# An R-GCN kernel on one core: sums for groups of 512 nodes held in PSUM, and row copies issued by SyncE alone

## The chip, the core and the metric

The kernel runs on one NeuronCore of one Trainium2 chip. The metric is the time of one execution in microseconds (us), taken on the device; ten runs are shown as a median with their lowest and highest. A profile is one further execution with every instruction recorded. Engines are named PE (TensorE, the matrix engine), DVE (VectorE), ACT (ScalarE), POOL (GpSimd) and SP (SyncE, which computes nothing and issues DMAs). L12 is line 12 of the kernel before, unless the text says "of the changed kernel".

## What is computed

Two layers of a relational graph convolution over 50,000 nodes with 128 features, then a residual and a layer norm. The 850,000 edges come sorted by destination; 50,000 of them are loops (one for each node, source equal to destination), so 800,000 join two nodes. Each edge has one of 16 relations, and a relation's 128x128 matrix is a mix of 8 bases.

```python
def _rgcn_layer(h, src, dst, rel, basis, w_comp, loop_w, bias):
    W = jnp.einsum('rb,bio->rio', w_comp, basis)
    seg = dst.astype(jnp.int32) * N_REL + rel.astype(jnp.int32)
    agg = jax.ops.segment_sum(h[src], seg, num_segments=N_ENT * N_REL)
    agg = agg.reshape(N_ENT, N_REL, -1)
    msg = jnp.einsum('nri,rio->no', agg, W)
    return jax.nn.relu(msg + h @ loop_w + bias)
h = _rgcn_layer(x, ...);  h = _rgcn_layer(h, ...)
x = _layernorm(x + h)
```

## The kernel before, in words

**Tiles and chunks.** The 800,000 edges are 6,250 tiles of 128 edges, and ten tiles (K = 10) make a chunk, so a layer has C = 625 chunks. The main loop (L925) goes over the chunks, once for each of the two layers (L854); the first layer reads `x`, the second reads `H1`, the first one's result in device memory.

**Source rows.** For each tile the 128 rows `h[src]` are brought into one of five chunk buffers `g` (GATHERS = 5) by an indirect DMA that POOL issues (`gather`, L202). In chunk c the gathers of chunk c + 2 are issued (L932 to L942). The first gather into a buffer waits until PE has read all of the chunk that was in it, five chunks earlier (`read_by`, L987).

**Tiles copied row by row.** The last tile of some chunks has no gather. Its 128 rows are copied by 128 single-row DMAs of 512 bytes (`row_by_row`, L789) into a buffer `by_hand`; the row addresses are loaded from a small table into an engine's registers, 16 at a time (L798). Two engines do this, each for every eighth chunk: SP for c % 8 = 7 and ACT for c % 8 = 3 (`HANDS`, L783; `by_hand`, L785). A copy is begun nine chunks before its chunk (L943 to L946) and issued in small portions behind the matmuls (L984 to L986).

**Sums by slot.** For each tile, DVE builds `hot` (L871): for each edge, its 8 basis weights at the place of its destination among 12 consecutive nodes ("slots"). PE multiplies the gathered rows by it (L971, `pa`), so a tile leaves 8 sums of 128 features for each of its 12 slots; ACT copies five tiles at a time from PSUM to `aT` (L979). Then PE multiplies by the eight bases and adds up in PSUM (`slots`, L734: eight matmuls of 120x128 a chunk), and ACT copies the result to SBUF (L739).

**From slots to nodes.** A window of 128 nodes, which begins at the chunk's first node, is taken for each chunk. PE adds the chunk's own slots and those of the chunk before by two 0/1 matrices (`masks_of`, L753; `nodes_of`, L761), DVE adds the nodes' own part `ls` (L764), which was stored to device memory earlier (L727) and is loaded again for the window (L883), and the window is finished and stored: relu on ACT (L768) in the first layer; in the second relu and residual in one DVE instruction with both tensors in SBUF (L771), then the norm (`normed_steps`, L601 to L614) and the store. A window's start is read from a register of SP (`at`, L627, with a load of 8 registers at L630).

**The own part.** `from_itself` (L692) does it for 128 nodes at a time: transpose (L209), two matmuls of 128x512 by the eight bases (L710), weights of the loops by DVE (L713), a matmul by the loop matrix (L722), the sum over nine terms on DVE (L726) and a store (L727).

**Preparing the edge lists.** During the first layer, DVE works through ten blocks of the edge list (`runs`, L310; `loops_of`, L415; `rows_of`, L442), a step or so for each chunk; two scatters for each block are issued by POOL (L378, L434).

**What sets the order.** PE, POOL, DVE and ACT run in the order in which the code is written (L853, `manual_schedule`). SP's order is made by a scheduler. A DMA issued by SP or ACT takes one of eight completion lanes in turn and waits until the DMA that had that lane before it has landed.

At the end a count that the kernel keeps of its own assumptions (`count_up`, L548) decides whether a slow general version (`summed`, L1028) is run as well.

Of the kernel before, what the change touches and what calls it, by code (L numbers as in the profile page):

```python
# [39 lines left out]
F32 = mybir.dt.float32  # L40
# [22 lines left out]
AHEAD = 4  # L63
# [8 lines left out]
BASES = 8  # L72
BY_HAND = 8
# [8 lines left out]
def tile_rgcn_resnorm(  # L82
# [21 lines left out]
    NG, NT = -(-R // P), -(-N // P)  # L104
# [9 lines left out]
    assert D == P and N >= P and edges.shape[0] == 1 and AT * NR == P and PER * NB * WN <= BANK and AT * PER * NB == WEIGHTS and PER == HALF and S <= P and C >= 4 and M > 0 and RUN - LK // 2 == LIVE and 2 * C <= NG * P and N <= 1 << 16 and E % ROW == 0  # L114
# [11 lines left out]
    NL = -(-(N + LK) // P) * P  # L126
    LREL = dram.tile([2 * NL, 1], I32, name="LREL")

    L = [dram.tile([N, D], F32, name=f"L{n}") for n in range(2)]
# [67 lines left out]
    ps_o = ctx.enter_context(tc.tile_pool(name="ps_o", bufs=1, space=PSUM))  # L197
    ps_n = ctx.enter_context(tc.tile_pool(name="ps_n", bufs=1, space=PSUM))
    ps_h = ctx.enter_context(tc.tile_pool(name="ps_h", bufs=2, space=PSUM))
# [6 lines left out]
    def turned(h, m, sb):  # L206

        tp = ps_o.tile([P, D], F32, name="po")
        nc.tensor.transpose(tp[:, :m], h, ident[:m, :m])  # L209
        hT = sb.tile([P, P], F32, name="hT")  # L210
        nc.scalar.copy(hT[:, :m], tp[:, :m])  # L211
        return hT[:, :m]
# [8 lines left out]
    key = consts.tile([P, 2 * C * HALF], BF16, name="key")  # L221


    base_i = consts.tile([1, C], I32, name="base_i")
    slot = consts.tile([P, C], F32, name="slot")
    next_slot = consts.tile([P, C], F32, name="next_slot")
    last_slot = consts.tile([P, 1], F32, name="last_slot")
    first_of = consts.tile([1, C], F32, name="first_of")
    base1 = consts.tile([1, C], F32, name="base1")
    minus = consts.tile([1, S], F32, name="minus")  # L230
# [4 lines left out]
    picked = consts.tile([P, 5 * NG + len(ROWS) + 4], F32, name="picked")  # L235
    ones = consts.tile([P, max(LIVE, C)], F32, name="ones")
# [10 lines left out]
    nc.vector.memset(minus, -1.0)  # L247
# [5 lines left out]
    def set_up(pool):  # L253
# [14 lines left out]
        po = ps_o.tile([P, D], F32, name="po")  # L268
# [146 lines left out]
    def loops_of(g, pool, m, d_i, k_f, r_i, loop, loops, asked):  # L415
# [15 lines left out]

        nc.vector.tensor_scalar(picked[0:1, 5 * g + 4 : 5 * g + 5], d_i[0:1, 0:1], float(asked()), None, op0=OP.is_ge)
        yield
# [8 lines left out]
    def rows_of(j, pool):  # L442
# [3 lines left out]
        parts = pool.tile([P, 2, LIVE, 2], F32, name="parts")  # L446
        for h in range(2):
            nc.sync.dma_start(
                parts[:m, h],
                FULL[h * NP + r0 * LIVE : h * NP + (r0 + m) * LIVE].rearrange("(p e) w -> p e w", e=LIVE),  # L450
            )
        if j:
            yield
        srcf = pool.tile([P, LIVE], F32, name="srcf")
        nc.vector.tensor_tensor(srcf[:m], parts[:m, 0, :, 0], parts[:m, 1, :, 0], op=OP.add)
        node = pool.tile([P, LIVE], I32, name="node")
        nc.vector.tensor_tensor(node[:m], parts[:m, 0, :, 1], parts[:m, 1, :, 1], op=OP.add)
# [19 lines left out]
        placed = put(srcf, src)  # L477
        row_at = pool.tile([P, LIVE], F32, name="real").bitcast(I32)[:, :P]
# [6 lines left out]
        keyf = pool.tile([P, LIVE], F32, name="keyf")  # L485
# [6 lines left out]
        if (r0 + m) * LIVE > M:  # L492
# [6 lines left out]
                beyond[:m], place[:m, :LIVE], last[:m], 64.0, op0=OP.subtract, op1=OP.mult  # L499
# [8 lines left out]
        po = ps_o.tile([P, D], F32, name="po")  # L508
# [6 lines left out]
        nc.vector.tensor_scalar(base1[:, c0 : c0 + cs], half[0:1, :, 0], float(N - P), None, op0=OP.min)  # L515
        nc.vector.tensor_scalar(base_i[:, c0 : c0 + cs], base1[:, c0 : c0 + cs], float(4 * D), None, op0=OP.mult)

        a, b = max(c0 - 1, 0), c0 + cs - 1
        off = pool.tile([1, P], F32, name="off")
        nc.vector.tensor_tensor(off[:, : b - a], base1[:, a + 1 : b + 1], base1[:, a:b], op=OP.subtract)  # L520
        yield
        po = ps_o.tile([P, D], F32, name="po")
        for h in range(2):
            nc.tensor.matmul(po[:S, :cs], spread[h], half[:, :, h], start=h == 0, stop=False)
        nc.tensor.matmul(po[:S, :cs], minus, base1[:, c0 : c0 + cs], start=False, stop=True)
        nc.vector.tensor_scalar(slot[:S, c0 : c0 + cs], po[:S, :cs], within[:S], None, op0=OP.add)
        yield
        po = ps_o.tile([P, D], F32, name="po")
        nc.tensor.matmul(po[:, : b - a], ones[0:1, :P], off[:, : b - a], start=True, stop=True)
        nc.vector.tensor_tensor(next_slot[:S, a:b], slot[:S, a:b], po[:S, : b - a], op=OP.subtract)  # L530
        if b == C - 1:
            nc.vector.tensor_tensor(
                last_slot[:S], next_slot[:S, b - 2 : b - 1], po[:S, b - a - 1 : b - a], op=OP.subtract
            )
# [6 lines left out]
            ones[:m, :LIVE],  # L541
# [6 lines left out]
    def count_up(pool):  # L548
        last = 5 * NG + len(ROWS)
        off = pool.tile([1, C], F32, name="off_all")  # L550

        nc.vector.memset(off, float(N - 1))
        nc.vector.tensor_copy(off[:, : C - 1], first_of[:, 1:])
        nc.vector.tensor_tensor(off, off, base1, op=OP.subtract)
        nc.vector.scalar_tensor_tensor(
            off, off, float(P - 1), ones[0:1, :C], op0=OP.is_le, op1=OP.mult, accum_out=picked[0:1, last : last + 1]
        )

        in_time = pool.tile([1, C], F32, name="in_time")
        nc.gpsimd.iota(  # L560
            in_time,
            pattern=[[P * NT // C, C]],
            base=P * AHEAD - P,
# [3 lines left out]
        nc.vector.tensor_tensor(off, base1, in_time, op=OP.subtract)  # L567
        nc.vector.scalar_tensor_tensor(
            off, off, 0.0, ones[0:1, :C], op0=OP.is_le, op1=OP.mult, accum_out=picked[0:1, last + 1 : last + 2]
        )  # L570

        nc.vector.tensor_tensor(off[:, : C - 3], base1[:, 2 : C - 1], first_of[:, 1 : C - 2], op=OP.subtract)
        nc.vector.tensor_tensor(off[:, C - 3 : C - 2], base1[:, C - 1 :], first_of[:, C - 3 : C - 2], op=OP.subtract)
        nc.vector.scalar_tensor_tensor(
            off[:, : C - 2],
            off[:, : C - 2],
            1.0,
            ones[0:1, : C - 2],
            op0=OP.is_ge,
            op1=OP.mult,  # L580
            accum_out=picked[0:1, last + 3 : last + 4],
        )
        nc.vector.tensor_scalar(picked[0:1, last + 2 : last + 3], first_of[:, 0:1], 0.0, None, op0=OP.is_equal)
# [3 lines left out]
        total = ps_o.tile([P, D], F32, name="po")  # L587
# [4 lines left out]
            off[:, 1:2], total[:1, 1:2], float(E + 2 * NG * (P + 1) + 3 * C - 1), None, op0=OP.not_equal  # L592
# [3 lines left out]
    def normed(t, m, sb):  # L596

        *_, o = normed_steps(t, m, sb)
        return o

    def normed_steps(t, m, sb):  # L601
        st = sb.tile([P, 6], F32, name="st")
        nc.vector.bn_stats(st[:m], t)  # L603
        mv = sb.tile([P, 2], F32, name="mv")
        nc.vector.bn_aggr(mv[:m], st[:m])  # L605
        sd = sb.tile([P, 1], F32, name="sd")
        nc.scalar.activation(sd[:m], mv[:m, 1:2], AF.Sqrt, bias=eps[:m])  # L607
        yield
        rs = sb.tile([P, 1], F32, name="rs")
        nc.vector.reciprocal(rs[:m], sd[:m])  # L610
        nm = sb.tile([P, 1], F32, name="nm")
        nc.vector.scalar_tensor_tensor(nm[:m], mv[:m, 0:1], -1.0, rs[:m], op0=OP.mult, op1=OP.mult)  # L612
        o = sb.tile([P, D], F32, name="o")
        nc.scalar.activation(o[:m], t, AF.Identity, bias=nm[:m], scale=rs[:m])  # L614
        yield o

    def chunked():
        with (
# [8 lines left out]
            def at(c):  # L627

                if c % BASES == 0:
                    _, starts[:] = nc.values_load_multi_w_load_instructions(  # L630
                        base_i[0:1, c : min(C, c + BASES)],
                        engines=[mybir.EngineType.SP],
                        min_val=0,
                        max_val=(N - P) * 4 * D,
                        skip_runtime_bounds_check_because="bases are clamped to N - P, and no node is below 0",
                    )
                return starts[c % BASES]

            def nodes_at(of, start):
                return of.bitcast(U8).rearrange("n d -> (n d)")[ds(start, P * 4 * D)].rearrange("(p d) -> p d", p=P)  # L640

            def weights(c, n):
# [9 lines left out]
                is_rel = hp.tile([P, LIVE], F32, name="is_rel")  # L652
# [14 lines left out]
            def loop_weights(i, n):  # L667

                m = min(AT, NT - i) * NR
                rel = hp.tile([P, 2, P], I32, name="lrel")  # L670
                for h in range(2):
                    nc.sync.dma_start(
                        rel[:m, h, :],
# [18 lines left out]
            def from_itself(i, of, n, lws):  # L692
# [8 lines left out]
                if i % AT == 0:  # L701
                    lws[:] = [next(weigh)]
# [512 lines left out]
```

## Time and profile before

| what | value |
|---|---|
| median of 10 runs | 15414.09 us (15409.94 to 15418.7) |
| the profiled execution: its own time | 15411.18 us |
| its span (first to last instruction) | 15409.4 us |
| granted TensorE clock, mean | 0.809 |
| busy: PE, DVE, ACT, POOL | 75%, 44%, 16%, 75% |
| gathers on POOL | 6,096 in each layer |
| row copies | 19,712 on SP and 19,712 on ACT |

In the profile a row of a group gives line, engine, operation, tiles (out<-in), shape, count, then the busy time and the mean duration of one, and behind the second bar the engine's idle time just ahead of these instructions and what ended it. "Issue" means that the engine waited for nothing that the profile shows. A fp32 matmul appears as two records, so a count of matmul records is twice that of the matmuls.

### The profile page before, as it was taken

How to read it: one execution, taken by the hardware profiler on the slowest of the kernel's cores; microseconds unless marked ns; L12 is line 12 of the kernel's file. 1: busy time of each engine (PE TensorE's matmuls, PEld its weight loads, DVE VectorE, ACT ScalarE, POOL GpSimd, SP SyncE). 2: the span in 40 equal slices, each digit the busy share in tenths (PEclk: the TensorE clock that was granted, in tenths of full speed). 3: DMA queues.
4: the chain of work that ended last, by engine and by line, in shares of the span. 5: the costliest groups of instructions: out<-in, count | busy, mean ns of one | idle time of the engine just before them, and what ended most of it. 6: DMA issues, size and time to landing. Idle time of an engine off the chain costs nothing. (4 is left out here: it accounts for less than half of the span.)

```text
span 15409.4 us, 255870 instructions
## 1 busy us (share of the span) xinstructions
PE 11590.4 (75%) x59202; PEld 9165.9 (59%) x59202; DVE 6777.2 (44%) x14585; ACT 2520.9 (16%) x6567; POOL 11585.2 (75%) x12224
## 2 busy tenths in 40 slices
PE   6777777776777777777777777777777777777777
PEld 4656555655666555556555555656666565656556
DVE  6544544445333333333344444444444444444444
ACT  1111111111111111111111111111111111111111
POOL 6777777777777777777777777777777777777777
PEclk8787787777788888888878888787787888888887
DMA  3333333333322222222223333333333333333332
GB/s 95 83 86 86 83 85 86 80 84 80 81 75 75 75 75 75 75 74 75 74 77 80 80 80 80 80 81 80 80 81 80 81 81 80 81 79 81 79 80 75
DMA packets 1236470, 1232.33 MB, mean 80 GB/s; under 512 B 318004, under 2 KB 1028332, under 8 KB 1234940
## 3 DMA queue, kind: packets, MB, share of 16 engines
q0 software_dynamic: 393696, 806.61, 20.9%
q1 hardware_dynamic: 798604, 397.62, 9.0%
q10 hardware_dynamic: 42640, 11.62, 0.3%
q8 instruction: 481, 7.88, 0.2%
q14 instruction: 1049, 8.59, 0.2%
HBM read 1059.71 MB, written 154.87 MB: 79 GB/s over the span
## 5 line engine op out<-in xcount | busy, mean ns | idle before, releaser
L971 PE MATMUL pa<-hot,g 128*128 128x96 f32 x24384 | 5933.2, 336 | 3358.3 <-DMA g<-H,src 1641.8
L971 PEld LDWEIGHTS pa<-hot,g 128*128 128x128 f32 x24384 | 4582.7, 233 | 5732.4 <-DMA g<-H,src 2272.6
L202 POOL DMA_INDIRECT g<-in_x_dram,src x6096 | 5793.6, 950 | 1891.3 <-issue 1811.9
L202 POOL DMA_INDIRECT g<-H,src x6096 | 5765.4, 946 | 1875.5 <-issue 1833.9
L734 PE MATMUL ps<-basis,aT 128*120 128x128 f32 x20000 | 3948.9, 332 | 0.0
L734 PEld LDWEIGHTS ps<-basis,aT 128*120 128x120 f32 x20000 | 3345.5, 235 | 0.0
L979 ACT COPY aT<-pa 128x480 f32<-128x480 f32 x2500 | 1395.4, 558 | 8242.0 <-DMA by_hand<-in_x_dram 3058.2
L713 DVE TENSOR_TENSOR by<-hb,lw 128x512 f32<-128x512 f32 x1564 | 1077.1, 689 | 3703.9 <-PE hb L710 3701.9
L710 PE MATMUL hb<-basis,hT 128*128 128x512 f32 x3128 | 2114.1, 765 | 4.2 <-ACT hT L211 4.2
L726 DVE TENSOR_REDUCE ls<-by 128x128 f32<-128x1152 f32 (+1 forms) x782 | 1657.2, 2119 | 13.5
L871 DVE TENSOR_TENSOR hot<-fixed,own 128x960 f32<-128x960 f32 x1250 | 1446.7, 1157 | 62.5 <-DVE own L864 1.8
L723 DVE TENSOR_TENSOR by<-po,bias 128x128 f32<-128x128 f32 (+1 forms) x782 | 227.2, 291 | 2257.6 <-PE po L722 2219.4
L761 PE MATMUL pn<-slots,own 120*128 120x128 f32 x5000 | 970.5, 326 | 31.8 <-DVE a L764 27.2
L761 PEld LDWEIGHTS pn<-slots,own 120*128 120x128 f32 x5000 | 817.1, 232 | 35.3 <-DVE a L764 29.9
L864 DVE TENSOR_TENSOR own<-fixed,key 128x120 f32<-128x120 f32 x1250 | 342.9, 274 | 1122.8 <-PE fixed L658 1104.3
L710 PEld LDWEIGHTS hb<-basis,hT 128*128 128x128 f32 x3128 | 598.7, 238 | 7.9 <-ACT hT L211 7.9
L607 ACT ACTIVATE sd<-mv,eps 128x1 f32<-128x1 f32 x625 | 184.1, 295 | 2377.3 <-DMA by_hand<-H 1768.5
L658 PE MATMUL fixed<-each,is_rel 128*128 128x64 f32 x3140 | 507.8, 323 | 4.0 <-DVE is_rel L653 4.0
L658 PEld LDWEIGHTS fixed<-each,is_rel 128*128 128x128 f32 x3140 | 489.6, 240 | 4.7 <-DVE is_rel L653 4.4
L209 PE MATMUL po<-ident,h_own 128*128 128x128 f32 (+1 forms) x782 | 271.5, 347 | 284.1 <-ACT lw L689 227.0
L614 ACT ACTIVATE o<-a,nm,rs 128x128 f32<-128x128 f32 x625 | 308.2, 493 | 961.9 <-DMA by_hand<-H 512.4
L753 DVE TENSOR_SCALAR own<-col,slot 120x128 f32<-120x128 f32 x1250 | 407.2, 326 | 0.0
(152 smaller groups left out, 4274.2 us busy)
## 6 DMA issues: line engine op xcount, KB each, us to landing
by_hand<-in_x_dram ACTq DMA_DIRECT2D x9856, 0.5 KB
by_hand<-in_x_dram SPq DMA_DIRECT2D x9856, 0.5 KB
by_hand<-H ACTq DMA_DIRECT2D x9856, 0.5 KB
by_hand<-H SPq DMA_DIRECT2D x9856, 0.5 KB
g<-in_x_dram,src POOLq DMA_INDIRECT x6096
g<-H,src POOLq DMA_INDIRECT x6096
ls_of<-L SPq DMA_DIRECT2D x1250, 64.0 KB
L<-ls SPq DMA_DIRECT2D x780, 64.0 KB
```

Of the source, the lines that this page charges most:

```text
L202: return nc.gpsimd.indirect_dma_start(out=to, out_offset=None, in_=of, in_offset=bass.IndirectOffsetOnAxis(ap=idx, axis=0))
L658: nc.tensor.matmul(of[:, :, j * NB : (j + 1) * NB], is_rel[:m, j * P : (j + 1) * P], EACH[n][:m], start=True, stop=True,)
L710: nc.tensor.matmul(hb[:m], hT, BASIS[n][:, b : b + few, :].rearrange("p b d -> p (b d)"), start=True, stop=True)
L713: nc.vector.tensor_tensor(by[:m, b : b + few, :], hb[:m].rearrange("p (b d) -> p b d", d=D), lw[:m, b : b + few, None].to_broadcast([m, fe ...
L726: nc.vector.tensor_reduce(ls[:m], by[:m].rearrange("p b d -> p d b"), AX.X, OP.add)
L734: nc.tensor.matmul(ps[: k * WN], aT[:, b, : k * WN], BASIS[n][:, b, :], start=b == 0, stop=b == NB - 1)
L753: nc.vector.tensor_scalar(own[:k], col[:k], at_node[:k], None, op0=OP.is_equal)
L761: nc.tensor.matmul(pn, own, st[i][: ks(i) * WN], start=j == 0, stop=j == len(masks) - 1)
L864: nc.vector.tensor_tensor(own[:, : ks(c)], grid[:, None, :].to_broadcast([P, ks(c), WN]), key[:, c * K : c * K + ks(c), None].to_broadcast ...
L871: nc.vector.tensor_tensor(hot[:, : ks(c)], pm[:, c % Q * K : c % Q * K + ks(c), :, None].to_broadcast([P, ks(c), NB, WN]), own[:, : ks(c), ...
L971: product = nc.tensor.matmul(pa[:, i * NB * WN : (i + 1) * NB * WN], g[:, k + i, :] if k + i < ks(c) - by_hand(c) else handed.pop(c), hot[ ...
L979: nc.scalar.copy(aT[:, :, k * WN : (k + m) * WN].rearrange("d b (i w) -> d i b w", w=WN), pa[:, : m * NB * WN].rearrange("d (i b w) -> d i ...
```

## The change

**Groups.** Nodes are taken in 98 groups of 512 (J = 4 nodes to a partition, 128 partitions). A group's sums stay in one PSUM bank (`sums`, `ps_n`) from the first to the last chunk that can hold an edge to it (`first`, `final`, L612 to L616 of the changed kernel). The two-chunk windows, the registers with their starts, and the store and reload of `ls` go. DVE spreads a chunk's slot sums over the four node places (`spread_out`, 512 wide), and PE adds them with a mask and a 512 wide matmul for each group that the chunk touches; the loop matrix is added into the same bank.

**Bases over four chunks.** `slots_of_batch` multiplies `aT` of four chunks at once by each basis (eight matmuls with 480 columns for four chunks in place of eight with 128 for each), then ACT copies and PE transposes back. The last chunks of a layer are done one at a time as before.

**Row copies.** A chunk's last tile is copied by hand where c % 5 = 4 and c is at least 8, by SP alone, begun eight chunks ahead, with 32 registers loaded at a time; ACT copies none.

The rest follows from these: own part, finish and norm work on a group of 512 (`from_itself`, `finish`, `normed`), one store for a group; `key` is held as 8-bit and `own` as bf16; the PSUM pools are divided anew; `count_up` checks other bounds.

```diff
-BY_HAND = 8
+BY_HAND = 5
+EARLY = 3
+OFFSETS = 32
...
-            HANDS = ((nc.sync, BY_HAND - 1), (nc.scalar, BY_HAND // 2 - 1))
...
-                return BY_HAND < c < C and ks(c) == K and any(c % BY_HAND == at for _, at in HANDS)
+                return ks(c) == K and c >= BY_HAND + EARLY and c % BY_HAND == BY_HAND - 1
...
+                        behind[:] = [nc.sync.dma_start(row, byte[None, ds(offsets[e % OFFSETS], 4 * D)]).ins]
...
+            def spread_out(c, of):
+                k = ks(c) * WN
+                st = sb.tile([P, J, D], F32, name="slots", bufs=BATCH)
+                nc.vector.tensor_tensor(
+                    st[:k],
+                    of[:k, None, :].to_broadcast([k, J, D]),
+                    which[:k, c, :, None].to_broadcast([k, J, D]),
+                    op=OP.mult,
+                )
...
+            def slots_of_batch(c, aT, st, n):
+                ps = ps_s.tile([P, BANK], F32, name="ps")
+                for b in range(NB):
+                    nc.tensor.matmul(
+                        ps[:, : BATCH * S], BASIS[n][:, b, :], aT[:, b, :], start=b == 0, stop=b == NB - 1
+                    )
...
+                nc.scalar.copy(by_slot, ps[:, : BATCH * S])
...
+                    nc.tensor.transpose(po[:S, q * P : (q + 1) * P], by_slot[:, q * S : (q + 1) * S], ident)
...
+                    nc.tensor.matmul(
+                        sums[g],
+                        own,
+                        of[:k].rearrange("s j d -> s (j d)"),
+                        start=c == first(g),
+                        stop=c == final(g),
+                    )
...
+                nc.vector.tensor_tensor(ls, sums.pop(g)[:m].rearrange("p (j d) -> p j d", j=J), ls, op=OP.add)
...
+                    nc.vector.scalar_tensor_tensor(ls, ls, 0.0, xws.pop(g)[:m], op0=OP.max, op1=OP.add)
```

## The prediction

> **What bounds the kernel now.** I read the page's busy times and slices first, then the gathers' rows, POOL's waits, and single instructions. The page:
>
> ```profile
> span 15409.4 us, 255870 instructions
> ...
> PE 11590.4 (75%) x59202; PEld 9165.9 (59%) x59202; DVE 6777.2 (44%) x14585; ACT 2520.9 (16%) x6567; POOL 11585.2 (75%) x12224
> ...
> L202 POOL DMA_INDIRECT g<-in_x_dram,src x6096 | 5793.6, 950 | 1891.3 <-issue 1811.9
> L202 POOL DMA_INDIRECT g<-H,src x6096 | 5765.4, 946 | 1875.5 <-issue 1833.9
> ```
>
> PE and POOL are both at 75%, so the shares do not decide. POOL's idle time does: nearly all of it is "issue", that is, nobody was waited for. The waits of POOL (total us, times, longest) say it more sharply:
>
> ```profile
> POOL g L202 <- issue: 3645.8, 11947, 0.3
> ...
> POOL g L202 <- DMA FULL<-full,to_i: 17.5, 1, 17.5
> POOL g L202 <- DMA H<-o: 15.7, 1, 15.7
> ...
> POOL g L202 <- PE pa L971: 7.9, 26, 0.3
> ```
>
> A pause of 3645.8 / 11947 = 0.305 us stands behind every gather, and POOL never waits for PE to free a buffer (longest 0.3, the ordinary pause). PE in turn waits for the gathers (the page has 3358.3 us idle ahead of L971). So POOL bounds the whole span, with one gather every 0.944 + 0.305 = 1.249 us; 0.944 is the median in the gathers' own view, whose lines also give minimum, maximum, first and last start:
>
> ```profile
> L202 POOL DMA_INDIRECT g<-in_x_dram,src x6096: 939/944/1628, 46.1 to 7746.2; - x197
> L202 POOL DMA_INDIRECT g<-H,src x6096: 940/944/1255, 7763.5 to 15387.8; - x197
> ```
>
> The span can be added up from this: first gather 46.1; 12,192 x 1.249 = 15,227.8; longer gathers, 5793.6 + 5765.4 - 12,192 x 0.944 = 49.8; the two waits 33.2; twenty scatters of POOL with their pauses some 31; from the last gather's end (15387.8 + 0.9) to the end 20.7. Together 15,409, the span. I work from the profiled execution, 15411.2, which is 1.8 above its span and 2.9 below the median of the runs.
>
> **The change, part by part.**
>
> *Row copies: fewer of them, so more gathers.* Before, c % 8 = 3 or 7 from 11 to 623 gives 154 tiles a layer; now c % 5 = 4 from 9 to 624 gives 124. Gathers go from 2 x (6,250 - 154) = 12,192 to 2 x (6,250 - 124) = 12,252, as the built order of POOL also has it. **60 more x 1.249 = +74.9 us**, all on the path, with no cover.
>
> *Longer gathers.* In layer 2 a gather takes 946 on average, in layer 1, with the edge blocks being prepared, 950. Some DVE instructions stretch gathers, and what they share is that both tensors come from SBUF: such as
>
> ```profile
> L771 DVE SCALAR_TENSOR_TENSOR a<-a,xw 128x128 f32<-128x128 f32 x625 | 183.8, 294 | 21.6
> L387 DVE SCALAR_TENSOR_TENSOR k_f<-loop_f 128x672 f32<-128x672 f32 x10 | 8.5, 845 | 0.0
> ```
>
> Between 4500 and 7500 us, where neither runs but all the DVE work on PSUM does (L713 of 689 ns, L871 of 1157 ns), the mean gather is 945. The preparation has some 15 such instructions of about 0.85 us for each of ten blocks; they hold most of layer 1's extra 950 - 946 = 4 ns x 6,096 = 24 us, so 24 / 150 = 0.16 us each, at most 36.6 / 150 = 0.24. The change drops L771's 625 short ones (at most all of layer 2's 12 us; I take -9) and brings 98 of the same operation on 512 elements (its line 823). Priced as the long ones: 98 x 0.2 = +20. Bounds: -9 (none stretches a gather) to +39 - 9 = +30 (0.4 each). I take **+11**, since 512 elements are nearer to 672 than to 128. The Trainium skill ("SBUF — State Buffer", section "Who interferes with whom") says that a DVE instruction with two SBUF inputs contends with a GpSimd instruction that reads SBUF, and that the later one blocks until the first ends; but it also infers that descriptor generation is not held by it. By the first, with the whole 0.69 us for each, the sum would be at most 48 us higher (an estimate); by the second, 11 lower. The rows above side with neither end.
>
> *Between the layers.* The first gather of layer 2 waits for the last store of H1, 16.3 us after the last gather. The new chain from that gather's end: landing 1.6, `pa` 0.3, three 512-wide mask matmuls that stand ahead 3.2 (1.05 each, a pair of L710 records in the timeline at 6015), eight base matmuls 2.5, spreading 0.7 (as L713), mask matmul 1.05, add 0.7, relu 0.6 (as L979), store 2.7 (from 7760.8 to 7763.5 now), hand-overs 1: 14.3; with L710's mean 1.53 for a wide matmul 16.2. I take **0**; bounds -3 and +5. The wait on FULL behind the last scatter stays.
>
> *The tail.* The same chain up to the add, 10.1 with its landing, then residual 0.7, four pairs of statistics 1.9, root, reciprocal and shift 0.6, four outputs of 0.49 on ACT, hand-overs 1, and 5.6 from the last output to the span's end as now: 22 against 20.7. **+2**, bounds -1 and +6.
>
> *At nothing, while POOL stays the bound.* On PE, base matmuls fall from 10,000 of 128 columns (0.31 us back to back) to 2,480 of 480 (0.98), and mask matmuls go from 2,500 narrow (0.32) to 2,064 wide (1.05), with 1,240 more transposes (0.35): -3,100 + 2,430 - 800 + 2,170 + 430 = +1,130, so PE goes from 75% to about 82%. DVE gets 1,250 spreadings (0.69) and loses 1,250 + 782 adds and 436 masks: +0.2 ms on 44%. ACT loses its copies. All of that sits beside the gathers. The cover is the five chunk buffers: POOL works up to about four chunks, 49 us, ahead of PE before a late PE stops it; beyond that each late us costs one.
>
> *SP is where that cover could fail.* The copies' issue, from SP's timeline, and its register loads of 16 and of 8:
>
> ```profile
> 5999.97 2.17 SPq L808 DMA_DIRECT2D by_hand<-in_x_dram  x7
> 6007.36 5.80 SPq L808 DMA_DIRECT2D by_hand<-in_x_dram  x16
> ...
> L798 SPq TENSOR_LOAD <-row_at x1232: 971/1169/3639, 159.6 to 15341.7; - x176
> ...
> L630 SPq TENSOR_LOAD <-base_i x158: 478/783/2112, 121.0 to 15387.6; - x158
> ```
>
> Seven in 2.17, one issue lasting 0.228: (2.17 - 0.228) / 6 = 0.324 us a row; sixteen in 5.80: 0.37, with waits for a lane. Loads: (1169 - 783) / 8 = 48 ns a register, so 1.94 for 32. In five chunks (49 gathers, 61.2 us) SP now issues 128 rows 41.5, four loads 7.8, other DMAs some 2.2: **51.5 of 61.2, 84%**; 57 with the slower rows. Before, its 128 rows were spread over eight chunks. Behind its waiting stores (one for a group now) and among its rows stand the loads that DVE and PE wait for, above all `rel` (80 KB for four chunks, now 413.9 us of waits in 55 cases, longest 16.1). In the built order of SP up to 230 rows and eight loads stand between two loads of `rel`: 90 us, where the pair ahead serves eight chunks, 98 us. So late loads must be expected, of tens of us, but mostly within the 49.
>
> **Sum:** 15411.2 + 74.9 + 11 + 0 + 2 = 15,499; in terms of the median +2.9: **15,502**. With the bounds of the small terms (-13 and +41 about their sum) 15,476 to 15,530.
>
> **The rivals.**
>
> 1. *SP too late.* Loads or rows come more than four chunks late, and POOL waits for PE. For it: 84% in order, with stores that wait; against: the rows have eight chunks, and their lanes are no longer shared with ACT's. SP becomes the bound outright when a row takes (61.2 - 10) / 128 = 0.40 us. At 0.43 each of the 248 tiles costs 3.8 us: +940, 16,440. Milder, late now and then, some 50 to 150 us: about 15,600.
>
> 2. *Not slower: the pitch falls.* ACT's 19,712 copies stop, and if they slow POOL's issue, each gather gains. Place: the 0.305 pause. To undo 75 + 13 us takes 88 / 12,252 = 7 ns a gather; 10 ns would be -123, 15,380. Against: before the first copy (up to 117 us) the median gather is already 944 and the pause 0.3, the same as with copies beside it.
>
> 3. *About the same.* The small terms all go the other way: no stretched gathers (-9 for +11), shorter chains at both layer ends (-3, -1). By my rows that still leaves 15,476, and within 31 us of 15,414 takes another 31, from a place that I cannot name.
>
> 4. *It does not do what it says.* If a bound in `count_up` were broken, the general version would run too, far beyond any time here.
>
> **How the numbers follow.** The forecast (POOL bounds, 60 more gathers) 0.80; rival 1 0.12, mostly its mild form; rival 2 0.03; rival 3 0.05; rival 4 below 0.01. The range takes the forecast's 15,476, 6 lower for the runs' spread, and reaches up through most of the mild form of rival 1: 15,470 to 15,590. A difference of about 0.2% (31 us) is what a measurement of this kernel can tell from none. Slower 0.92, same 0.05, faster 0.03.
>
> **What would show it.** Right: 12,252 gathers with a median of 944 and a pause of 0.3; POOL's waits on PE `pa` never over 0.3; layer 2's mean gather near 948 with the long ones under the new line 823; SP's waits on stores still there (it has time left). Wrong: POOL waiting for `pa` of the changed kernel's line 1023, DVE waiting long for `rel`, rows at 0.4 us; or a pause below 0.3.

## The result, and the profile after

| | kernel before | changed kernel |
|---|---|---|
| median | 15,414.1 us (15,409.9 to 15,421.8, 28 runs) | 15,500.9 us (15,499.0 to 15,504.5, 8 runs) |
| ratio, with its 95% interval | | 1.0056 (1.0047 to 1.0065) |
| the profiled execution | 15,411.2 | 15,494.5 |
| gathers | 12,192 | 12,252 |

The change costs 86.8 us by the medians, 83.3 by the profiled executions. Forecast were 15,502 and +88. Every line number from here on, unless said otherwise, is one of the kernel whose lines are shown.

The page of the changed kernel, its span, busy times and the rows of the gathers (busy, mean ns, then the idle time ahead of them):

```profile
span 15492.7 us, 191120 instructions
...
PE 12023.4 (78%) x45072; PEld 7318.9 (47%) x45072; DVE 6722.2 (43%) x11506; ACT 1939.1 (13%) x3706; POOL 11645.7 (75%) x12285
...
L206 POOL DMA_INDIRECT g<-in_x_dram,src x6126 | 5818.5, 950 | 1898.8 <-issue 1797.1
L206 POOL DMA_INDIRECT g<-H,src x6126 | 5800.8, 947 | 1885.5 <-issue 1825.1
```

The gathers' own view (minimum, median, maximum ns; first and last start):

```profile
L206 POOL DMA_INDIRECT g<-in_x_dram,src x6126: 940/944/2152, 46.7 to 7778.8; - x198
L206 POOL DMA_INDIRECT g<-H,src x6126: 940/944/1450, 7798.0 to 15465.8; - x198
```

And POOL's waits (total us, times, longest):

```profile
POOL g L206 <- issue: 3622.2, 11821, 17.6
...
POOL g L206 <- PE pa L1023: 33.6, 110, 0.3
```

The reader is to see three things. The median gather is 944 ns as before, and so is the pause, although ScalarE's copies are gone: the 17.6 in the line of 3622.2 us is the one wait between the layers, and (3622.2 - 17.6) / 11,820 is 0.305 us. POOL still never waits for PE: 0.3 us is the ordinary pause. And the gathers of layer 2 are a little longer, 947 ns against 946. POOL with its fixed pitch is the bound, as before, and it has 60 gathers more to issue.

What did change is a wait off the path. DVE waits longer for the relation numbers that SP loads (413.9 us in 55 cases before):

```profile
DVE is_rel L632 <- DMA rel<-REL: 881.8, 113, 28.5
```

### The profile page after: what moved, and what is told of

Its sections match the earlier page's. It is cut to its first block, busy times and chain, and to the rows that moved or that the text cites. A ratio compares the mean times of both kernels' runs of the same rounds, so it can differ in the third digit from the quotient of the medians.

```text
span 15492.7 us, 191120 instructions
## 1 busy us (share of the span) xinstructions
PE 12023.4 (78%) x45072; PEld 7318.9 (47%) x45072; DVE 6722.2 (43%) x11506; ACT 1939.1 (13%) x3706; POOL 11645.7 (75%) x12285
## 4 chain that ended last, share of the span: by engine, by line
POOL 50%; issue 24%; SPq 10%; DMA 7%; PE 6%; DVE 2%; ACT 0%; POOLq 0%; ACTq 0%; DVEq 0%
POOL g L206 50%; SPq L859 8%; DMA g<-in_x_dram,src 3%; DMA g<-H,src 3%; SPq L851 2%; PE pa L1023 2%; PE pn L796 1%; PE po L710 1%; PE ps L754 1%; DMA lrel<-LREL 0%; PE po L670 0%; DMA rel<-REL 0%; DMA parts<-FULL 0%; DVE ls L725 0%; PE fixed L637 0%
## 5 line engine op out<-in xcount | busy, mean ns | idle before, releaser
L1023 PE MATMUL pa<-hot,g 128*128 128x96 f32 x24504 | 5251.3, 319 | 2630.6 <-DMA g<-in_x_dram,src 1341.9
L206 POOL DMA_INDIRECT g<-in_x_dram,src x6126 | 5818.5, 950 | 1898.8 <-issue 1797.1
L206 POOL DMA_INDIRECT g<-H,src x6126 | 5800.8, 947 | 1885.5 <-issue 1825.1
L796 PE MATMUL pn<-slots,own 120*128 120x512 f32 x4128 | 2676.2, 774 | 76.4 <-DVE slots L742 75.5
L754 PE MATMUL ps<-aT,basis 128*128 128x480 f32 x4960 | 2670.8, 622 | 16.8 <-ACT aT L1031 15.8
L717 DVE TENSOR_TENSOR by<-po,lw 128x512 f32<-128x512 f32 x1568 | 1074.8, 687 | 2978.2 <-PE po L710 2962.4
L710 PE MATMUL po<-basis,hT 128*128 128x512 f32 x3136 | 1931.0, 702 | 172.3 <-DVE by L717 171.9
L742 DVE TENSOR_TENSOR slots<-po,which 120x512 f32<-120x512 f32 x1240 | 780.1, 680 | 1389.7 <-PE po L764 1362.7
L906 DVE TENSOR_TENSOR own<-fixed,key 128x120 bf16<-128x120 f32 x1250 | 343.0, 274 | 1304.9 <-PE fixed L637 1294.4
L754 PEld LDWEIGHTS ps<-aT,basis 128*128 128x128 f32 x4960 | 811.6, 206 | 33.4 <-ACT aT L1031 31.7
L710 PEld LDWEIGHTS po<-basis,hT 128*128 128x128 f32 x3136 | 544.8, 218 | 200.8 <-DVE by L717 199.9
L779 DVE TENSOR_SCALAR own<-col,node 120x128 f32<-120x128 f32 x2064 | 542.9, 304 | 13.6 <-PE pn L796 13.6
```

Source lines behind the costliest of these rows:

```text
L206: return nc.gpsimd.indirect_dma_start(out=to, out_offset=None, in_=of, in_offset=bass.IndirectOffsetOnAxis(ap=idx, axis=0))
L710: nc.tensor.matmul(hb[:m], hT[:, j, :m], BASIS[n][:, b : b + few, :].rearrange("p b d -> p (b d)"), start=True, stop=True,)
L717: nc.vector.tensor_tensor(by[:m, b : b + few, :], hb[:m].rearrange("p (b d) -> p b d", d=D), lw[:m, j, g % T, b : b + few, None].to_broadc ...
L742: nc.vector.tensor_tensor(st[:k], of[:k, None, :].to_broadcast([k, J, D]), which[:k, c, :, None].to_broadcast([k, J, D]), op=OP.mult,)
L754: nc.tensor.matmul(ps[:, : BATCH * S], BASIS[n][:, b, :], aT[:, b, :], start=b == 0, stop=b == NB - 1)
L796: nc.tensor.matmul(sums[g], own, of[:k].rearrange("s j d -> s (j d)"), start=c == first(g), stop=c == final(g),)
```

## The experiments

The comparisons below are with a run of the kernel before on the same chip; "+n" is the difference of the medians to that. The changed kernel stands at +87.

### No copies at all

```diff
-                return ks(c) == K and c >= BY_HAND + EARLY and c % BY_HAND == BY_HAND - 1
+                return False
```

> The changed kernel without any copied rows: every tile is gathered by POOL, 12,500 gathers instead of 12,252. Theory (POOL's gathers alone set the time, copies cost POOL nothing): 248 x 1.249 = +309.8 us against the changed kernel's 15,501, so 15,811; the median gather stays 944 and the pause behind it 0.305. Rival (row copies slow POOL's issue, so that without them each gather is 7 ns shorter): 309.8 - 12,500 x 0.007 = +222, 15,723. Rival (SP's lateness holds the changed kernel up by some 50 us): 15,760. Below 15,770 speaks against the theory.

Measured: 15,802.8 us, +391, so 305 over the changed kernel. The groups of its gathers:

```profile
L206 POOL DMA_INDIRECT g<-in_x_dram,src x6250 | 5935.6, 950 | 1934.8 <-issue 1822.0
L206 POOL DMA_INDIRECT g<-H,src x6250 | 5921.1, 947 | 1921.6 <-issue 1834.0
```

The means are those of the changed kernel to the ns. By spans the difference is 15,800.8 - 15,492.7 = 308.1, that is 1.242 us for each of the 248 gathers, against 1.249 forecast. So a copied tile costs POOL nothing and saves it one gather with its pause. The two rivals (15,723 and 15,760) are out.

### The kernel before with SyncE's copies alone

```diff
-            HANDS = ((nc.sync, BY_HAND - 1), (nc.scalar, BY_HAND // 2 - 1))
+            HANDS = ((nc.sync, BY_HAND - 1),)
```

> The kernel before with SyncE's copies left (chunks c % 8 = 7) and ScalarE's taken away: 77 copied tiles a layer instead of 154, 12,346 gathers instead of 12,192. Everything else as before. Theory (each tile that goes back to POOL costs one gather with its pause): 154 x 1.249 = +192 us, 15,606. Rival (ScalarE's copies slowed POOL, so that their end gives 7 ns a gather): +192 - 86 = +106, 15,520.

Measured: 15,597.7 us, +186, which is 1.21 us for each of the 154 tiles that went back to POOL. ScalarE's 19,712 copies had not slowed POOL by anything like 7 ns a gather: here the gathers' time over their median is 5864.0 + 5834.7 - 12,346 x 0.944 = 44 us against 50 before, 0.5 ns a gather, and the pause behind a gather, counted in the two traces, is 304.9 ns on average against 305.2. The rival (15,520) is out.

### The other half alone: new groups, old copies

The changed kernel with two copiers as in the kernel before; `row_by_row` gets the engine as an argument.

```diff
-BY_HAND = 5
+BY_HAND = 8
...
+            HANDS = ((nc.sync, BY_HAND - 1), (nc.scalar, BY_HAND // 2 - 1))
...
-                return ks(c) == K and c >= BY_HAND + EARLY and c % BY_HAND == BY_HAND - 1
+                return ks(c) == K and c >= BY_HAND + EARLY and any(c % BY_HAND == at for _, at in HANDS)
```

> The changed kernel (groups of 512, bases over four chunks) with the copies of the kernel before: SyncE in the chunks c % 8 = 7, ScalarE in those of c % 8 = 3, 154 tiles a layer, 12,192 gathers as before. It is the other half of the change alone. Theory (the copies' count is nearly the whole change): 15,501 - 60 x 1.249 = 15,426, that is +12 against the kernel before (longer gathers, layer ends). Rival (SyncE and ScalarE hold each other up in the new order of work, since their rows are handed out in turn): above 15,460, with POOL waiting for PE `pa`.

Measured: 15,423.4 us (ratio 1.0009, interval 1.0000 to 1.0018), +13. With the old number of gathers the whole regrouping (groups of 512, bases over four chunks) is worth 13 us; the other 74 of the 87 come with the 60 gathers, 1.23 each. The interval leaves from 0 to 28 us for the 13. The rival (above 15,460) is out, and the change splits as it was forecast.

It also shows where the late loads of the changed kernel come from. With 19,712 rows on SP in place of 31,744, DVE's wait for `rel` is all but gone:

```profile
DVE is_rel L632 <- DMA rel<-REL: 2.1, 1, 2.1
```

### The residual step with one tensor in PSUM

In layer 2 the add writes the group's sum back to its PSUM bank, and the 512 wide instruction reads it from there.

```diff
-                nc.vector.tensor_tensor(ls, sums.pop(g)[:m].rearrange("p (j d) -> p j d", j=J), ls, op=OP.add)
+                total = sums.pop(g)[:m].rearrange("p (j d) -> p j d", j=J)
+                nc.vector.tensor_tensor(ls if n == 0 else total, total, ls, op=OP.add)
...
-                    nc.vector.scalar_tensor_tensor(ls, ls, 0.0, xws.pop(g)[:m], op0=OP.max, op1=OP.add)
+                    nc.vector.scalar_tensor_tensor(ls, total, 0.0, xws.pop(g)[:m], op0=OP.max, op1=OP.add)
```

> The changed kernel with only this different: in layer 2 the group's sum is written back to PSUM, and the residual step (512 elements, 98 times) reads its one tensor from PSUM and x from SBUF, instead of both from SBUF. Theory (two SBUF inputs stretch the gather beside them): by the price of the prediction -20 us, by the trace of the changed kernel -13 (98 x 0.13): 15,481 to 15,488, and the sum of POOL's gather times in layer 2 falls by that, its mean from 947 to 945. Rival (the stretch has another cause): 15,501, mean gather unchanged at 947.

Measured: 15,480.9 us, +69, that is 17 less than the changed kernel by the medians and 13.6 by the spans. The gathers:

```profile
L206 POOL DMA_INDIRECT g<-in_x_dram,src x6126 | 5816.2, 949 | 1898.7 <-issue 1800.6
L206 POOL DMA_INDIRECT g<-H,src x6126 | 5789.8, 945 | 1885.9 <-issue 1825.8
```

Layer 2 falls by 11.0 us, from 5800.8 to 5789.8, and its mean from 947 to 945. (Layer 1, where the edit changes nothing, moved by 2.3.) The rival (no change) is out. Counted gather by gather in the traces: in the changed kernel the gathers that overlap one of the 98 residual steps last 12.7 us longer than 944 ns each would make, 0.13 us for each step; here they last 0.0 longer. Beside the add, whose output the edit also moved, they are 0.0 longer in both.

The 0.13 is an average of two cases. In the changed kernel 49 gathers are stretched: those that start at least 0.06 us after the start of a step of 0.69 us and before its last 0.13 us. Each of them is held until the step ends: if the step ends at T after the gather's start, the gather takes T - 0.127 us more than 0.944 (to within 6 ns in all 49), at most 0.506 us more. Gathers that start before a step, or up to 0.04 us after its start, are not longer at all. This is where the Trainium skill bears on the result: "SBUF — State Buffer", section "Who interferes with whom", has a DVE instruction with two SBUF inputs contend with GpSimd's reads of SBUF, as an exclusive lock, and infers for `tensor_tensor` that descriptor generation is spared. The 49 gathers, which read their row numbers from `src` in SBUF, agree with the lock. That a gather which has had its first 0.13 us is no longer held fits the inference, but no row tells the reading of the numbers from the making of the descriptors.

### Three chunk buffers instead of five

```diff
-GATHERS = 5
+GATHERS = 3
```

> The changed kernel with three chunk buffers instead of five: POOL may run two chunks, 24.5 us, ahead of PE instead of four. In the changed kernel's trace PE is behind the gathers by over 24.5 us in 13 of 1,250 chunks, in seven groups whose highest excesses add up to 42 us. Theory (the late loads are real, the five buffers hide them): +42 us, 15,543 (15,520 to 15,580), with POOL waiting for PE `pa` a few times, some us to 13 us each. Rival (PE's lateness is an effect of POOL's running ahead and vanishes with it): 15,501.

Measured: 15,527.0 us, +117, 30 over the changed kernel. POOL's waits now have the line that was to be looked for:

```profile
POOL g L206 <- PE pa L1023: 77.4, 145, 12.7
```

145 ordinary pauses of 0.3 are 44 of the 77.4; some 34 us are real waits, the longest 12.7. So the late loads do put PE behind by more than two chunks now and then, and the five buffers do hide them. The forecast of +42 counted PE's lateness from the end of a chunk's last gather. Counted in the same trace from the start of the gather three chunks on, which is the one that has to wait, the worst excesses of the seven groups add up to 32.

### SyncE in every fourth chunk

```diff
-BY_HAND = 5
+BY_HAND = 4
```

> The changed kernel with SyncE copying the last tile of every fourth chunk instead of every fifth: 155 tiles a layer, 12,190 gathers, 62 fewer. SyncE's issue in four chunks: 128 rows of 0.323 (41.3 us), four loads of 2.13 (8.5), other DMAs some 1.8: 51.6 us, against 39 gathers or 48.7 us of POOL. Theory of rival 1's point (SyncE becomes the bound where its issue exceeds POOL's time): 2 x 625 / 4 x 51.6 and some 80 at the ends = about 16,200 (15,900 to 16,600), with POOL waiting for PE `pa`. Against it (SyncE still has room): 15,501 - 62 x 1.249 = 15,424.

Measured: 17,372.9 us (ratio 1.127), against 15,424 if SP had room. The chain that ended last, by engine, then DVE's wait for `rel` on the page, and lines of waits:

```profile
SPq 62%; issue 15%; PE 13%; DMA 4%; DVE 3%; POOL 1%; ACT 0%; DVEq 0%; ACTq 0%; POOLq 0%
```

```profile
L632 DVE TENSOR_SCALAR is_rel<-rel,its_rel 128x640 f32<-128x640 uint8 x314 | 181.8, 579 | 4766.5 <-DMA rel<-REL 4766.4
```

```profile
POOL g L206 <- PE pa L1023: 1895.1, 326, 26.7
```

```profile
PE po L695 <- DMA h_own<-H: 1788.2, 59, 40.3
PE pn L796 <- DVE slots L742: 1732.4, 80, 53.4
```

SP is the bound, the loads behind its rows come late, DVE and PE wait for them and POOL for PE: rival 1, whole. It is dearer than expected by 1,170 us. The sum of SP's time, from the start of each of its instructions to the next, counted in the traces, says why (us):

| kernel | work: rows x 0.323, loads of registers, other DMAs | waits inside the rows | other waits | sum |
|---|---|---|---|---|
| changed kernel | 10,253 + 2,189 + 671 = 13,113 | 425 | 1,950 | 15,488 |
| every fourth chunk | 12,817 + 2,792 + 671 = 16,280 | 378 | 708 | 17,366 |
| new groups, old copies | 6,367 + 1,391 + 1,124 = 8,882 | 4,270 | 2,265 | 15,417 |
| ScalarE every tenth too (below) | 10,253 + 2,325 + 723 = 13,301 | 3,795 | 232 | 17,328 |

The work is what was expected (16,280 for 16,200). The 1,086 of waits were left out: SP works in order, so even when it is the bound it still waits, 336 us of it for the tensors that it stores. By this, as an estimate, the changed kernel has 15,493 - 13,113 - 1,086 = 1,294 us to spare, 0.041 on each of 31,744 rows: SP would be the bound from 0.364 us a row on, not from 0.40.

### ScalarE as a second copier

First in every fifth chunk beside SP, then in every tenth, with the residual step in PSUM as well. The first of them:

```diff
+            HANDS = ((nc.sync, BY_HAND - 1), (nc.scalar, BY_HAND // 2))
...
+                return ks(c) == K and c >= BY_HAND + EARLY and any(c % BY_HAND == at for _, at in HANDS)
...
-                        behind[:] = [nc.sync.dma_start(row, byte[None, ds(offsets[e % OFFSETS], 4 * D)]).ins]
+                        behind[engine] = engine.dma_start(row, byte[None, ds(offsets[e % OFFSETS], 4 * D)]).ins
```

> The changed kernel with ScalarE as a second copier: it copies the last tile of the chunks c % 5 = 2 from 12 on, as SyncE does those of c % 5 = 4. 12,006 gathers, 246 fewer than in the changed kernel. Theory (POOL bounds, both copiers have time left): -246 x 1.249 = -307 us, 15,194. Rival (ScalarE's register loads and rows hold up the copies out of PSUM, so that PE falls behind by more than the chunk buffers cover): between 15,194 and 15,501, with POOL waiting for PE `pa`. Rival (copies by ScalarE lengthen POOL's pause): 15,194 plus 12 us for each ns.

Measured: 17,825.7 us (ratio 1.157). The theory fell, and both rivals with it: neither reaches this time, and the gathers keep their median of 944 ns. ScalarE waits ahead of its copies out of PSUM, not for PE but for rows:

```profile
ACT aT L1033 <- DMA by_hand<-in_x_dram: 6544.2, 1052, 27.3
ACT aT L1033 <- DMA by_hand<-H: 6364.4, 1039, 18.7
ACT aT L1033 <- PE pa L1025: 1111.1, 241, 16.6
```

I then took this for a limit on all rows together: 63,232 rows in some 17,600 us are 0.279 each, and I used 0.277. The second run was to test that.

```diff
+            HANDS = ((nc.sync, 5, 4), (nc.scalar, 10, 2))
...
+                return ks(c) == K and any(c >= every + EARLY and c % every == at for _, every, at in HANDS)
```

> The changed kernel with ScalarE as second copier in every tenth chunk (c % 10 = 2, from 22 on, 61 tiles a layer) beside SyncE's every fifth, and with the residual step reading its sum from PSUM. 12,130 gathers, 122 fewer than in the changed kernel. With a copier each for every fifth chunk the rows of both together took 70 us for 256, 0.277 each, and POOL waited. Here 192 rows x 0.277 = 53 us in five chunks, of 60.6 that POOL takes. Theory (that limit of all rows together decides): there is room, 15,501 - 152 - 20 = 15,329. Rival (any copying by ScalarE beside SyncE's every fifth chunk holds PE up, since ScalarE's rows wait in order for SyncE's): above 15,400, with POOL waiting for PE `pa`.

Measured: 17,341.6 us (ratio 1.125), so 69 us for the 192 rows of five chunks, 0.36 each. That theory fell too: no fixed pace of rows. The rival held (above 15,400, with POOL waiting 1,873 us for `pa`). SP's own waits show what took the place of the pace:

```profile
SPq L861 <- DMA by_hand<-H: 1712.6, 1684, 54.4
SPq L861 <- DMA by_hand<-in_x_dram: 1622.2, 1700, 12.4
```

SP now waits 3,335 us for rows ahead of its rows, and in the table its other waits are down to 232: it has no time left, with hardly more work than in the changed kernel. Rows of both engines take the eight completion lanes in turn, so a row of SP can wait for one of ScalarE. The trace tells who had the lane before: of SP's waits of over 0.3 us ahead of a row, 3,186 us stand behind a row of ScalarE, and in 658 of them, 2,226 us, ScalarE had not yet issued that row when SP was ready for its own. For 1,241 of these 2,226 us ScalarE stood mainly ahead of an `aT` copy, for which it waits for PE. PE in turn waits for DVE (2,431 us ahead of L710), and DVE for what SP loads. So the three wait for one another in a ring, and the chain that ended last passes through it; the page:

```profile
PE 32%; SPq 27%; DMA 16%; issue 9%; DVE 9%; ACTq 4%; ACT 1%; POOL 1%; DVEq 0%; POOLq 0%
...
L632 DVE TENSOR_SCALAR is_rel<-rel,its_rel 128x640 f32<-128x640 uint8 x314 | 178.8, 569 | 4848.7 <-DMA rel<-REL 4848.7
```

The new groups with the old copies have the same kind of wait (1,925 us in 478 cases) and bear it, since SP has 2,265 us of other waits to spend. A run with separate lanes for the two engines was not made, and what exactly paces the first run, with ScalarE in every fifth chunk, stays open. SP at 85% of its time bears 61 tiles of ScalarE a layer no better than 31 more of its own. The Trainium skill ("Perfetto Trace Analysis", section "DMA Optimizations") says that balancing DMAs over the engines that can issue them may help when descriptor generation is the bottleneck. Here it depends on the time that the issuers have left: both copiers at every eighth chunk (15,423) do better than SP alone at every fifth (15,501), and a second issuer beside the latter makes it worse.

### Two copiers farther apart, on other chips

New groups, the residual step in PSUM, and both copiers at every eighth, seventh and sixth chunk.

> The changed kernel with the copies of the kernel before (SyncE c % 8 = 7, ScalarE c % 8 = 3), and the residual step reading its sum from PSUM. Theory (the two effects add up): 15,423 with the old copies, less 98 x 0.13 to 0.2 = 13 to 20 us: 15,403 to 15,410, that is no measurable difference from the kernel before. Rival (the residual step's gain depends on the copies): 15,423.

> The changed kernel with SyncE copying in the chunks c % 7 = 6 and ScalarE in those of c % 7 = 3, and the residual step reading its sum from PSUM. About 88 tiles a layer for each copier, 354 in all, so 12,146 gathers: 106 fewer than in the changed kernel. Theory (the two copiers hold each other up only once little time is left over: 256 rows at 0.277 are 71 us, of 68 x 1.249 = 85 in seven chunks): 15,501 - 132 - 20 = 15,349, faster than both kernels. Rival (the two queues are over the edge already, as with ScalarE's every tenth chunk beside SyncE's every fifth): above 15,450, with POOL waiting for PE `pa` for hundreds of us.

> The same kernel as the earlier one with both copiers in every seventh chunk (176 tiles a layer, 12,148 gathers, 104 fewer than in the changed kernel) and the residual step reading its sum from PSUM, because that run was on a chip where the kernel before itself took 21,052 us. Theory (on a chip where the kernel before takes 15,41x, two copiers at this spacing have time left): 15,501 - 130 - 20 = 15,351. Rival (two copiers are over the edge at this spacing): above 15,450, with POOL waiting for PE `pa`.

> The same with both copiers in every sixth chunk: SyncE c % 6 = 5, ScalarE c % 6 = 3, 206 tiles a layer, 12,088 gathers, 164 fewer than in the changed kernel. POOL takes 58 x 1.249 = 72.4 us for six chunks; 256 rows at the 0.277 measured with both copiers at every fifth take 71. If only that limit decided: 15,501 - 205 - 20 = 15,276. Since SyncE and ScalarE also wait in order for other work, I expect it over the edge: 16,000 to 18,500, with POOL waiting for PE `pa`.

| copies | this kernel | kernel before, same chip | ratio |
|---|---|---|---|
| every 8th | 19,655.6 | 21,052.2 | 0.934 (0.932 to 0.935) |
| every 7th | 20,369.8 | 21,052.2 | 0.968 (0.966 to 0.970) |
| every 7th, again | 20,341.0 | 20,964.3 | 0.971 (0.969 to 0.972) |
| every 6th | 21,413.8 | 20,964.3 | 1.022 (1.021 to 1.024) |

The first two rows are from one chip and the last two from another; on both, the kernel before itself took 36% longer than on the chips of all other runs. None of the expectations can be judged by it. Of the new variants there, the more copies, the slower; the gathers keep their median of 944 ns in the one with every 8th chunk. With as many copies as the kernel before, that variant is 1,397 us faster than it, where on an ordinary chip the new groups with the old copies were 13 us slower. A burst of SP's rows in the timeline (start, length, rows) of the kernel with every 8th chunk:

```profile
8000.38 6.54 SPq L861 DMA_DIRECT2D by_hand<-in_x_dram  x5
```

and in the kernel with the new groups and old copies, on the ordinary chip:

```profile
6007.91 4.06 SPq L860 DMA_DIRECT2D by_hand<-in_x_dram  x9
```

Some 1.5 us a row against 0.5 in these two; over all 19,712 rows of SP the median from one to the next is 0.49 us there and 0.33 here, and 3,118 follow the one before by 1.35 to 1.52 us there, 48 here. Why SP is slow on those chips is open. So is whether the two copiers at every seventh chunk would beat the kernel before on the ordinary chips, and how the changed kernel itself fares on the others: neither was measured. On the ordinary chips no variant was faster than the kernel before; nearest came the new groups with the old copies (15,423).

## Why the prediction was right

**The bound.** POOL's gathers at a fixed pitch, with nothing else on the path: median 944 and pause 0.305 in the changed kernel, and 1.21 to 1.24 us for each gather added or taken away in three runs.

**60 more gathers, +74.9.** The run with the new groups and the old copies puts it at 74 by the medians. Right.

**Longer gathers, +11.** Measured +3.6: 5818.5 + 5800.8 - 12,252 x 0.944 = 53.4, against 49.8. It is +7.1 in layer 2 and -3.4 in layer 1, where nothing was forecast. The cause was right, and three sizes were off. The 98 long instructions cost 12.7 us, 0.13 each, where the estimate took 0.2 from the 672 wide ones. The short ones that went were worth some 7 us, counted in the same way, where the estimate took 9. (Of the sums behind these prices, "all of layer 2's 12 us" is 10.8 by the row, and the 36.6 of layer 1 is 39.0.) A price per instruction cannot be carried over from another length in proportion: a gather is held only if it starts between 0.06 us after the start of the instruction and 0.13 us before its end, and then until that end. For starts spread evenly over the pitch this gives, as an estimate, (0.69 - 0.19)^2 / (2 x 1.249) = 0.10 us for the new ones, where 0.13 was counted, and 0.17 for the 672 wide ones of 0.845 us. The bounds (-9 to +30) held the sum.

**Between the layers, 0.** Measured +1.9: 7798.0 - 7778.8 - 0.9 = 18.3 against 7763.5 - 7746.2 - 0.9 = 16.4. Inside -3 to +5.

**The tail, +2.** Measured +5.3: 15,492.7 - 15,466.7 = 26.0 against 20.7. Inside its bounds, at their end. The step that was short is "the same chain up to the add, 10.1": the add ended 15.9 us after the last gather. DVE's timeline shows one of the two things left out:

```profile
15478.87 0.69 DVE L823 SCALAR_TENSOR_TENSOR ls<-ls,xw 128x512 f32<-128x512 f32 x1
15479.60 0.29 DVE L584 BATCH_NORM_STATS2 st<-ls 128x6 f32<-128x128 f32 x1
...
15481.86 0.16 DVE L592 SCALAR_TENSOR_TENSOR nm<-mv,rs 128x4 f32<-128x4 f32 x1
15481.94 0.68 DVE L817 TENSOR_TENSOR ls<-pn,ls 84x512 f32<-84x512 f32 x1
```

The last add (L817) stands behind the residual and the statistics of the group before; PE had finished its sum at 15479.42, so this is 2.5 us. The other: a second set of wide mask matmuls (2.8 us from 15472.99) stands on PE between the last tile's product and its bases. What follows the add took 10.1 us where 11.9 were forecast, which hid part of the miss.

**At nothing, while POOL stays the bound.** PE came to 78% instead of 82%, and its waits stay within the buffers. The cover was real and was needed: with three buffers instead of five it fails by 30 us. "Late loads of tens of us, mostly within the 49" is what the traces show: `rel` up to 28.5, and `lrel`, which the prediction did not look at, up to 42.0; PE behind the gathers by up to 37 us.

**SP at 84%.** Work 13,113 of 15,493 is 85%. The row at 0.323 was right; the load of 32 registers took 2.13 us instead of the 1.94 extrapolated. Its waits on stores, the sign that it has time left, were there:

```profile
SPq L821 <- ACT ls L820: 691.1, 71, 32.4
```

What failed is the point from which rival 1 decides: "a row takes 0.40" counts SP's work alone. With the waits that SP keeps when it is the bound, it is, by the estimate above, nearer to 0.36, and one step farther on this road, every fourth chunk, costs 1,870 us.

**Rival 2** (the pitch falls with ScalarE's copies) is refuted by the median of 944 and by the kernel before without them: 0.5 ns a gather, not 7. **Rival 3** needed the small terms to fall together; they rose by 3.6 + 1.9 + 5.3 = 10.8.

**Luck.** The bound and the 60 gathers were right by their mechanism. That the forecast of 15,502 came within 2 us of the median is luck: the small terms were forecast at 13 in all and came to 10.8, with the longer gathers 7.4 too high and the two layer ends 5.2 too low.

## What to carry to other kernels

When one engine paces the whole span with a fixed pitch, count what the change adds to and takes from that engine first: here 60 instructions explained 74 of 87 us, and a large regrouping of the other engines' work 13. When work is concentrated on one in-order DMA queue, add the waits that it will still have to its work before calling the rest room: 85% of work was fine, and every fourth chunk, 106% by the sum of its work, took 113% of POOL's time. A second queue does not simply add to the first while their transfers take the same completion lanes in turn: each then waits for the other's place in its own order, and needs time to spare for it.

## What the runs showed of the hardware

- A DVE instruction of 0.69 us with both tensors in SBUF holds a gather that starts behind it until it has ended (49 gathers, up to 0.506 us late, 0.13 us for each of the 98 instructions). A gather that starts first is not held, and the same instruction with one tensor in PSUM holds none.
- A row copy waits for the DMA that had its completion lane before, the other engine's too: 2,226 us in 658 cases in which ScalarE had not yet issued that DMA when SP was ready.
- Single-row DMAs by ScalarE or SyncE do not slow POOL's gathers measurably (0.5 ns of 1,249 for 19,712 of them).
- On two chips the kernel before ran at 21.0 ms where the others gave 15.4: the time of such a kernel can depend on the chip far more than on the change. The cause was not found.
